# Two transformer layers on one core: feed-forward products from two 12-bit float32 parts, the value matrix laid out through DRAM, the ternary weights prepared first

## The chip, the cores and the metric

The kernel runs on one core of one Trainium2 chip. The metric is the device time of one execution in microseconds (us), lower is better. A core has a matrix engine (TensorE, PE in the profile; PEld is its weight load, which runs beside the products), a vector engine (VectorE, DVE), an engine for activation functions and copies (ScalarE, ACT), GpSimd (POOL), and SyncE (SP), which here issues all DMA transfers. Work lies in SBUF, 128 partitions wide; products land in PSUM, eight banks of 128 x 512 float32.

## What is computed

Sixteen batches of 256 tokens with 256 features pass through two layers. After each of the four sublayers the input is added and the sum is normalised (`x = _layernorm(x + f(x))`):

```python
# 1: mixing in the Fourier domain, 16 heads of 16
qf, kvf = fft(x @ W_q.T), fft(x @ W_kv.T)          # each divided by its norm
values = ifft(qf * cumsum(kvf, axis=1)).real;  out = values @ W_o.T
# 2: eight small experts, the best one of each token by a gate
out = (1 - sel_scale) * x + sel_scale * (bias + degen_up)
# 3: attention, 16 heads of 16; the 256 x 768 projection is only reshaped to (3, 16, 256, 16)
Q, K, V = (x @ W_qkv.T).reshape(b, 3, H, L, D_H)   # per batch
out = softmax(Q @ K.T / 4) @ V @ W_o.T
# 4: feed-forward, 1024 wide, with weights rounded to three levels in groups of 64
w1, w2 = ternary(W_fc), ternary(W_proj)
h = square(relu(x @ w1.T));  out = (h * rsqrt(mean(h**2) + eps)) @ w2.T
```

Three levels times a bfloat16 scale: each weight of the fourth sublayer has few significant bits. Inputs, outputs and all matrix products of the kernel before are float32.

## The kernel before

Sublayers 1 and 2 of a batch are `front`, sublayer 4 is `back`. Attention runs for four batches at a time: `attention(i)` for the groups i = 0 to 3, batch g of a group on the partitions 32g to 32g+15.

The order of the instructions is made when the program is built. Every operation is entered with the tiles that it reads and writes, a cost in us for each engine that may do it, and a priority (`order.prio`; a smaller number goes first). A planner (`Order.run`) keeps a clock for every engine, takes at each step the operation that can start earliest, among near equals the one with the smaller priority, gives it a buffer, and fixes its place in its engine's queue. Every engine then runs its queue in that order. Buffers are few: eight PSUM banks (at most six for attention, two for the work beside it), thirteen 512-wide `work` tiles, four `x` tiles for the inputs.

The main loop first folds the Fourier matrices into the projections (`fold`, L417 to L451), then runs the four fronts of group 0. For each group it then enters the attention of group i, and beside it the four backs of group i-1 and the four fronts of group i+1, which fill gaps. After group 0's attention has been entered, `ternaries` (L465 to L489) turns the two feed-forward weights into three levels; its loads wait for `begun`, a mark that a score product of group 0 sets. The last four backs come at the end.

`attention` in steps: the projection products (L759) into a bank, for blocks of 32 tokens. VectorE transposes each block (L768) into the tile `zt`, whose three thirds are Q, K and V; the marks `zq`, `zr`, `zv` and `turn` stand for those parts and for the turn of the group. A row of ones is written beside K by DMA (L776). V is turned once more on TensorE (L793) and evacuated into `v`, 32 columns a head and batch, zeros in the unused ones (L342 and L343, the shared evacuation on ScalarE or VectorE). First pass: scores (L810), whose row maxima VectorE takes (L819); a DMA writes the maxima beside Q (L827). Second pass, head by head: scores with the maxima subtracted (L844), the exponential on ScalarE into tiles in the V third of `zt` (L853), the products with V (L859), then transpose, division and store into `o` (L867, L871). At the end the output projection (L901).

`back`: the input is transposed on TensorE (L521) and evacuated. The first product (L925) goes into a bank in four parts of two blocks of 128; each part passes through relu (L933), a square (L936 on ScalarE or L937 on VectorE), and a second square for the mean (L941). VectorE sums the second squares over the eight blocks in one reduction (L949). The second product (L959) has the transposed hidden values as its stationary operand; a product with a column of ones (L968) sums the squares over the partitions. Normalisation (from L535) and the output DMA (L983) follow.

Of the kernel before, what the change touches and what calls it, by code (L numbers as in the profile page):

```python
# [11 lines left out]
BF16 = mybir.dt.bfloat16  # L12
AF = mybir.ActivationFunctionType
# [17 lines left out]
ZQ = H * S  # L31
LN_EPS = 1e-5
# [5 lines left out]
C_ALL = C_INV + 2 * 2 * P  # L38


def constants():
# [12 lines left out]
    inv = np.zeros((2, HD, 8))  # L54
    for k in range(8):
# [5 lines left out]
        inv[1, :, k] = (1 + alt) / 16 if k == 0 else -si / 16  # L61
        c[k::8, C_MK : C_MK + 3] = (0, 0, 1) if k == 0 else (1, -1, 0)
    ft = np.zeros((H, HD, 2, H, 8))
    iv = np.zeros((2, H, HD, H, 8))
# [4 lines left out]
    iv = iv.reshape(2, 2, P, P)  # L69
    for e in range(2):  # L70
        c[:, C_FT + e * 256 : C_FT + (e + 1) * 256] = ft[e]
        for m in range(2):
            at = C_INV + (m * 2 + e) * P
            c[:, at : at + P] = iv[m, e]
# [11 lines left out]
LAG = {PE: 0.27, DVE: 0.2, ACT: 0.25, POOL: 0.2, SP: 2.4}  # L86
SLACK = {PE: 0.15, DVE: 0.1, ACT: 0.1, POOL: 0.1, SP: 0.0}
SWITCH = 0.13
LATER = 15.0
# [46 lines left out]
class Order:  # L136
# [65 lines left out]
    def run(self):  # L202
# [5 lines left out]
        clock = {e: 0.0 for e in LAG}  # L208
        mode = None
# [3 lines left out]
        while ready:  # L213
# [42 lines left out]
            clock[e] = at + (cost if e != SP else 0.06)  # L256
# [18 lines left out]
def forward(ctx, tc, x, xt, wq, wkv, wo0T, f0, degen, cs, wqkvT, wo1T, wfc, wproj, cst, out):  # L275
# [3 lines left out]
    pp = ctx.enter_context(tc.tile_pool(name="pp", bufs=1, space=PSUM))  # L279
    order = Order(tc)  # L280
# [13 lines left out]
    zq, zv, zr = fixed(zt_), fixed(zt_), [fixed(zt_), fixed(zt_)]  # L294
    begun = fixed(zt_)
# [4 lines left out]
    at = 3328  # L300
# [3 lines left out]
    for i in range(13):  # L304
        order.slot("work", place(f"work{i}", [P, 512]))
    for i in range(2 * GB):
        order.slot("x2", place(f"x2_{i}", [P, 512]))
    for tag, bufs, n in (
        ("x2T", 1, 2 * GB * S), ("x", 4, 512), ("h", 1, 2048), ("sq", 1, 2048), ("oT", 1, 2048), ("pd", 3, 512), ("f", 2, 272), ("c2", 2, 128),
        ("mk", 1, 144), ("mT", 1, 256), ("st", 34, 16), ("st64", 6, 64), ("nm", 2, 64), ("nmT", 2, 128),  # L310
    ):
        for i in range(bufs):
            order.slot(tag, place(f"{tag}{i}", [P, n]))
    for i in range(2):
        order.slot("wb", place(f"wb{i}", [P, 512], BF16))
        order.slot("sb", place(f"sb{i}", [P, 8], BF16))
    order.slot("lane", *[None] * 4)
    order.limit = {("ps", "r"): 2, ("ps", "a"): 6, ("lane", "r"): 2}
    v = const("v", [P, 2 * H, GB, 32])
    o = const("o", [P, S // 32, D])  # L320


    def load(dst, src, dst_tile, prio=None):
        return op((SP, 0.1, lambda: nc.sync.dma_start(dst(), src)), [dst_tile], [], prio=prio)
# [37 lines left out]
    wqs = fixed(zt_[:, 1280:2304].rearrange("p (s c d) -> p s c d", s=2, c=2))  # L362
    wos = fixed(zt_[:, 2304:2816].rearrange("p (c d) -> p c d", c=2))
    f0s = fixed(zt_[:, 2816:3104].rearrange("p (c f) -> p c f", c=2))
    rows = fixed(zt_[0:NE, 3104:3240])
# [688 lines left out]
```

## Time and profile before

| What | us |
|---|---|
| Median of three runs (932.14, 940.5, 941.45) | 940.5 |
| Profiled execution, its own time | 940.41 |
| Its span, first to last instruction | 938.6 |
| Fronts of group 0 end, the projection of group 0 begins | 106.3 |
| Projection of groups 1, 2, 3 begins | 310.0, 487.3, 694.7 |
| Output projection of group 3 begins | 863.7 |

A row of the profile's groups names a line of the kernel, an engine, an operation, the tile written and the tiles read with their shapes, the number of instructions, their busy time together, the mean time of one in ns, and the idle time of the engine just before them with what ended it. Instructions of one engine overlap, so the mean of one can be longer than the busy time divided by the count. A release by "issue" is time in which the engine waited for nothing that the profile shows. The granted clock (PEclk) is the share of TensorE's full clock that the chip allowed.

### The profile page before, as it was taken

Reading aid. Unit: us, or ns where it says so; the run is one execution under the profiler, and the core shown is the slowest. Engines: PE = TensorE matmul, PEld = TensorE weight load, DVE = VectorE, ACT = ScalarE, POOL = GpSimd, SP = SyncE. Lnnn points to the kernel's source line nnn. Section 1 sums busy time; section 2 is a strip of 40 time slices with the busy share of each in tenths; the row PEclk is TensorE's granted clock in tenths of the full one; section 3 lists DMA queues with packets and bytes.
Section 4 is the critical chain, followed back from the end, with each engine's and each line's share of the span. In section 5 each row is a group of like instructions: output and inputs, shape, how many; then the busy total and the mean of one; then the engine's idle time right before and its main releaser. Section 6 shows DMA issues by size and latency. Waiting matters only on the chain.

```text
span 938.6 us, 14746 instructions
## 1 busy us (share of the span) xinstructions
PE 870.9 (93%) x5678; PEld 609.5 (65%) x5678; DVE 662.6 (71%) x1449; ACT 425.9 (45%) x845; POOL 146.1 (16%) x334
## 2 busy tenths in 40 slices
PE   7777999949899999999989999999999999999996
PEld 4554678525568676676556777766667778545885
DVE  1868799897577998858659898566689794313553
ACT  4826110536646213675661435495632226454542
POOL 1122100365112001012102001012120001000201
PEclk9978795578899998999999999999999899656998
DMA  5101030000000000011000000000000000000000
GB/s 181 54 12 45 2 96 11 2 1 2 22 23 13 11 15 14 13 35 36 12 13 3 1 25 25 1 24 12 2 1 4 2 14 24 12 1 1 1 23 23
DMA packets 18874, 19.01 MB, mean 20 GB/s; under 512 B 2092, under 2 KB 17780, under 8 KB 18804
## 3 DMA queue, kind: packets, MB, share of 16 engines
q1 hardware_dynamic: 18804, 18.07, 6.4%
q8 instruction: 44, 0.72, 0.3%
q14 instruction: 26, 0.21, 0.1%
HBM read 13.35 MB, written 4.19 MB: 19 GB/s over the span
## 4 chain that ended last, share of the span: by engine, by line
PE 79%; DVE 13%; ACT 5%; issue 1%; POOL 1%; DMA 0%; DVEq 0%; SPq 0%; ACTq 0%; POOLq 0%
PE bank L925 13%; PE bank L959 11%; PE bank L759 9%; PE bank L810 8%; PE bank L844 7%; PE bank L859 7%; PE bank L575 5%; PE bank L654 3%; PE bank L901 3%; DVE nm L819 3%; PE bank L521 3%; DVE work L949 2%; PE bank L731 2%; PE bank L620 2%; PE bank L675 1%; PE bank L793 1%
## 5 line engine op out<-in xcount | busy, mean ns | idle before, releaser
L853 ACT ACTIVATE zt<-bank 128x512 f32<-128x512 f32 x256 | 135.3, 607 | 91.9 <-PE bank L844 91.8
L819 DVE TENSOR_REDUCE nm<-bank 128x2 f32<-128x512 f32 x256 | 157.4, 680 | 12.6 <-PE bank L810 12.2
L959 PE MATMUL bank<-w2T,h 128*128 128x256 f32 x512 | 120.9, 387 | 2.6 <-DVE work L738 2.6
L925 PE MATMUL bank<-work,w1T 128*128 128x256 f32 x512 | 121.6, 390 | 1.4 <-ACT work L342 1.4
L529 POOL TENSOR_SCALAR st<-st 128x2 f32<-128x2 f32 x80 | 17.1, 214 | 609.7 <-DVE st L537 388.0
L959 PEld LDWEIGHTS bank<-w2T,h 128*128 128x128 f32 x512 | 96.0, 192 | 21.9 <-issue 4.3
L925 PEld LDWEIGHTS bank<-work,w1T 128*128 128x128 f32 x512 | 96.7, 194 | 20.4 <-issue 2.4
L844 PE MATMUL bank<-zt 17*128 17x256 f32 x1024 | 101.0, 488 | 6.7 <-ACT zt L853 5.8
L810 PE MATMUL bank<-zt 16*128 16x256 f32 x1024 | 97.1, 457 | 0.4 <-DVE nm L819 0.4
L859 PE MATMUL bank<-zt,v 128*32 128x256 f32 x1024 | 94.2, 478 | 3.3 <-ACT zt L853 3.3
L844 PEld LDWEIGHTS bank<-zt 17*128 17x128 f32 x1024 | 63.8, 229 | 41.0 <-issue 21.3
L933 ACT ACTIVATE work<-bank 128x512 f32<-128x512 f32 x64 | 37.9, 594 | 115.4 <-PE bank L925 115.3
L768 DVE STREAM_TRANSPOSE zt<-bank 128x1024 f32<-128x1024 f32 x64 | 84.4, 1447 | 7.4 <-PE bank L759 7.4
L759 PE MATMUL bank<-wqr,x2T 128*128 128x512 f32 (+1 forms) x256 | 83.7, 487 | 0.0
L810 PEld LDWEIGHTS bank<-zt 16*128 16x128 f32 x1024 | 67.5, 210 | 24.6 <-issue 13.4
L759 PEld LDWEIGHTS bank<-wqr,x2T 128*128 128x128 f32 x256 | 48.9, 191 | 33.7 <-issue 30.3
L859 PEld LDWEIGHTS bank<-zt,v 128*32 128x32 f32 x1024 | 33.9, 127 | 48.9 <-issue 30.6
L949 DVE TENSOR_REDUCE work<-sq 128x256 f32<-128x2048 f32 x16 | 59.1, 3696 | 7.1 <-ACT sq L941 7.1
L575 PE MATMUL bank<-wf,x 128*128 128x512 f32 x128 | 60.8, 611 | 0.1
L867 DVE STREAM_TRANSPOSE work<-bank 128x512 f32<-128x512 f32 x32 | 22.6, 708 | 52.8 <-PE bank L859 52.8
L530 POOL TENSOR_TENSOR st<-st,mhalf 128x2 f32<-128x2 f32 x80 | 57.1, 716 | 5.4
L535 DVE BATCH_NORM_STATS2 st<-work 128x6 f32<-128x256 f32 x120 | 45.2, 414 | 0.4
(171 smaller groups left out, 1164.8 us busy)
## 6 DMA issues: line engine op xcount, KB each, us to landing
x<-in_xT SPq DMA_DIRECT2D x16, 256.0 KB, 2.8
x<-in_x SPq DMA_DIRECT2D x16, 256.0 KB, 2.8
out<-work SPq DMA_DIRECT2D x16, 256.0 KB, 2.1
work<-in_wfc SPq DMA_DIRECT2D x4, 256.0 KB, 4.4
work<-in_wproj SPq DMA_DIRECT2D x4, 256.0 KB, 5.5
wqr<-in_wqkvT SPq DMA_DIRECT2D x1, 768.0 KB, 6.6
zt<-in_cst SPq DMA_DIRECT2D x1, 512.0 KB, 3.9
zt<-nmT SPq DMA_DIRECT2D x32, 8.0 KB, 1.8
```

Source lines behind the costliest of these rows:

```text
L530: pool([dst], [dst, mhalf], 0.7, lambda: G.tensor_tensor(dst.v, dst.v, a(mhalf)[:, 0:n], ALU.pow))
L575: T.matmul(pb.v.rearrange("p a s k -> p (a s k)"), xT.v[:, c, ts(t, P)], a(wf)[:, c].rearrange("p a s f -> p (a s f)"), start=(c == 0), st ...
L759: T.matmul(b.v.rearrange("p j d -> p (j d)"), x2T.v[:, c, tb].rearrange("p g k -> p (g k)"), a(wqr)[:, c, j0 * HD : (j0 + nj) * HD], start ...
L768: lambda b=b, tb=tb, j0=j0, nj=nj: V.transpose(ztv[:, j0 : j0 + nj, ts(tb, 32)], b.v.unsqueeze(2).to_broadcast([P, nj, 2, HD])),
L810: T.matmul(sc[g].v[:, t, :], part(g, HD, 0, h, t * P, P), part(g, HD, 1, h), start=True, stop=True,)
L819: lambda nm=nm, sc=sc, g=g, h=h: V.tensor_reduce(nm.v[:, g, h % 8, :], sc[g].v, AX.X, ALU.max, negate=True),
L844: T.matmul(sc[g].v[:, c, :], part(g, HD + 1, 1, h, c * P, P), part(g, HD + 1, 0, h), start=True, stop=True,)
L853: act([e], [sc[g]], 512, lambda e=e, sc=sc, g=g: A.activation(e.v, sc[g].v, AF.Exp, scale=HD ** -0.5))
L859: T.matmul(av.v[32 * g : 32 * g + 32, hk, :], a(v)[:, h * 2 + c, g, :], es[g].v[:, c, :], start=(c == 0), stop=(c == 1),)
L925: T.matmul(pb.v[:, i, :], a(w1T)[:, c, ts(q * 2 + i, P)], xT.v[:, c, :], start=(c == 0), stop=(c == 1))
L949: (DVE, 2.2, lambda: V.tensor_reduce(acc.v, sq.v.rearrange("p k s -> p s k"), AX.X, ALU.add)),
L959: T.matmul(pw.v[:, t, :], h.v[:, k, ts(t, P)], a(w2T)[:, k, :], start=(k == 0), stop=(k == HID // P - 1))
```

## The change

Float32r is a type of 32 bits of which the matrix engine takes a shortened mantissa; the change declares the feed-forward weights and four new tiles in it.

- **Feed-forward.** The input and the hidden values are each split into a high part (a copy into a float32r tile) and a low part (the value minus the high part). Each product becomes two, one with each part, summed in the same bank. The second squares are added part by part into one tile, then halves are added, in place of the one reduction. `h`, `sq` and one `work` tile give way to `xs`, `hi` and `lo`.
- **V.** Only the blocks up to the sixth are still transposed into `zt`. The blocks from the sixth on are evacuated into a `work` tile, written to DRAM by SP (six writes a group), and read back by SP into `v` in its final layout (four reads a group, pieces of 16 values). The turn on TensorE is gone, `v` has 17 columns a head and batch, and the projections of the last two blocks no longer wait for the group's turn, at a priority 2 lower.
- **Ternary weights.** Entered before the first attention, in tiles that share memory with `o` and `oT`; their loads have priority -8.5, ahead of `wqr` and `wo1`. GpSimd takes no part; the steps that subtracted and added the weight again are gone; a maximum is joined to a multiplication.
- **Prologue.** Two loads of constants in place of one, all four transposed inputs first, the untransposed inputs of group 0 not loaded; nine products on a tile of ones at the start (`warm`); `fold` in two parts with two more matrices. The early fronts form two products in place of the masked ones and add the input, and the bias of the gate, on TensorE.
- **Planner.** New costs for DMA issue and transfer, for some VectorE operations, and for the new products.

```diff
-LAG = {PE: 0.27, DVE: 0.2, ACT: 0.25, POOL: 0.2, SP: 2.4}
+LAG = {PE: 0.27, DVE: 0.2, ACT: 0.25, POOL: 0.2, SP: 0.3}
...
+ISSUE = 0.43
+MOVE = 1.2
...
-            clock[e] = at + (cost if e != SP else 0.06)
+            clock[e] = o.end
+            if e == SP:
+                clock[e] = at + ISSUE
+                o.end = moved = max(at + ISSUE + 1.6, moved + cost)
...
-    for i in range(13):
+    for i in range(12):
         order.slot("work", place(f"work{i}", [P, 512]))
...
+    for i in range(2):
+        order.slot("xs", place(f"xs{i}", [P, 2 * 512], F32R))
+    for tag in ("hi", "lo"):
+        order.slot(tag, place(tag, [P, 2048], F32R))
...
-    w1T, w2T = const("w1T", [P, 2, HID]), const("w2T", [P, HID // P, D])
+    w1T, w2T = fixed(place("w1T", [P, 2, HID], F32R)), fixed(place("w2T", [P, HID // P, D], F32R))
...
+    def warm():
+        b = ps([P, P], "p")
+        def go():
+            for n in range(9):
+                T.matmul(b.v, a(ones), a(ones), start=True, stop=True)
+        pe([b], [ones], 2.5, go, prio=-20.0)
...
+        if early:
+            one, two = w(P, 2, S), w(P, 2, S)
+            dve([one], [qT, cu, *extra], 512, lambda: V.tensor_tensor(one.v, qT.v, cu.v, ALU.mult))
+            dve([(two, 0)], [qT, cu, *extra], 256, lambda: V.tensor_tensor(two.v[:, 0, :], qT.v[:, 0, :], cu.v[:, 1, :], ALU.mult))
+            dve([(two, 1)], [qT, cu, *extra], 256, lambda: V.tensor_tensor(two.v[:, 1, :], qT.v[:, 1, :], cu.v[:, 0, :], ALU.mult))
...
+                    for n, (l, g) in enumerate((
+                        (one.v[:, 0, at], a(gi)[:, 0, :]), (one.v[:, 1, at], a(ge)[:, 0, :]),
+                        (two.v[:, 0, at], a(ge)[:, 1, :]), (two.v[:, 1, at], a(ge)[:, 1, :]),
+                    )):
+                        T.matmul(y.v[:, t, :], l, g, start=(n == 0), stop=False)
+                    for c in range(2):
+                        T.matmul(y.v[:, t, ts(c, P)], xT.v[:, c, at], ident, start=False, stop=(c == 1))
...
+                if tb >= 5:
+                    st = tile_("work", [P, nj * HD])
+                    evacuate(lambda st=st: st.v, lambda b=b: b.v.rearrange("p j d -> p (j d)"), st, b, nj * HD)
+                    op(
+                        (SP, 0.1, lambda st=st, tb=tb, j0=j0, nj=nj: nc.sync.dma_start(
+                            vd.slot.ap[:, tb * 32 - VT : tb * 32 - VT + 32, j0 * HD : (j0 + nj) * HD], st.v
+                        )),
+                        [(vd, (tb, j0))], [st],
+                    )
+        for g in range(GB):
+            op(
+                (SP, 0.1, lambda g=g: nc.sync.dma_start(
+                    va[:, :, g, 0:HD],
+                    vd.slot.ap[g].rearrange("t e -> (t e)")[2 * ZQ * HD - VT * NJ * HD :].rearrange("(n p d) -> p n d", p=P, d=HD),
+                )),
+                [(v, g)], [vd],
+            )
...
+        act([(xs, 0)], [bx], 512, lambda: A.copy(xs.v[:, 0], bx.v))
+        dve([(xs, 1)], [bx, (xs, 0)], 512, lambda: V.tensor_tensor(xs.v[:, 1], bx.v, xs.v[:, 0].bitcast(F32), ALU.subtract))
...
-                    for c in range(2):
+                    for n in range(4):
                         T.matmul(
-                            pb.v[:, i, :], a(w1T)[:, c, ts(q * 2 + i, P)], xT.v[:, c, :], start=(c == 0), stop=(c == 1)
+                            pb.v[:, i, :], a(w1T)[:, n // 2, ts(q * 2 + i, P)], xs.v[:, n % 2, n // 2, :],
+                            start=(n == 0), stop=(n == 3),
                         )
...
+            act([(hi, q)], [h], 512, lambda h=h, part=part: A.copy(part(hi), h.v))
+            act([sq], [h], 512, lambda h=h, sq=sq: A.activation(sq.v, h.v, AF.Square))
+            dve([(lo, q)], [h, (hi, q)], 512, lambda h=h, part=part: V.tensor_tensor(part(lo), h.v, part(hi).bitcast(F32), ALU.subtract), us=0.69)
+            if q:
+                dve([acc], [acc, sq], 512, lambda sq=sq: V.tensor_tensor(acc.v, acc.v, sq.v, ALU.add), us=0.69)
...
+                        for n, part in enumerate((hi, lo)):
+                            T.matmul(
+                                pw.v[:, t, :], part.v[:, k, ts(t, P)], a(w2T)[:, k, :],
+                                start=(k + n == 0), stop=(k + n == HID // P),
+                            )
...
+    order.prio = 90.0
+    ternaries()
     for i in range(NG):
         order.prio = 100.0 * (i + 1)
         attention(i)
-        if i == 0:
-            order.prio = 105.0
-            ternaries()
```

## The prediction

> **What bounds the kernel now.** I read the page's engine line first, then the busy time of each engine by stage (the cuts lie where the first projection product of each group of four batches starts, and where its score passes begin and end), then the groups of instructions, the timeline of the tail, ten-microsecond windows for the clock, and the DMA queues.
>
> ```profile
> span 938.6 us, 14746 instructions
> ## 1 busy us (share of the span) xinstructions
> PE 870.9 (93%) x5678; PEld 609.5 (65%) x5678; DVE 662.6 (71%) x1449; ACT 425.9 (45%) x845; POOL 146.1 (16%) x334
> ```
> TensorE leaves 67.7 us of the span idle; VectorE is second. By stage (columns: length, busy time of PE, PEld, DVE, ACT, POOL with counts, granted clock, DMA share, GB/s):
>
> ```profile
> core 0: us, PE busy (x) PEld busy (x) DVE busy (x) ACT busy (x) POOL busy (x), PEclk, DMA share, GB/s
> 14.30:106.30 92.00, 71.56 (x268) 48.67 (x268) 63.43 (x216) 49.82 (x101) 15.96 (x41) 0.84 0.11 32
> 106.30:184.00 77.70, 77.38 (x490) 54.36 (x490) 72.23 (x114) 14.57 (x33) 6.56 (x5) 0.70 0.11 33
> 184.00:224.00 40.00, 25.38 (x204) 14.32 (x206) 38.94 (x62) 18.26 (x34) 28.50 (x25) 0.71 0.01 1
> 224.00:310.00 86.00, 80.56 (x519) 58.14 (x512) 57.50 (x177) 51.97 (x105) 16.21 (x49) 0.93 0.06 16
> 310.00:487.30 177.30, 170.44 (x1264) 114.69 (x1263) 138.41 (x307) 88.52 (x181) 20.03 (x54) 0.97 0.07 20
> 487.30:694.70 207.40, 202.58 (x1444) 144.40 (x1443) 157.90 (x358) 103.13 (x209) 31.94 (x92) 0.99 0.04 11
> 694.70:804.80 110.10, 109.85 (x675) 81.86 (x673) 83.50 (x114) 34.77 (x65) 7.47 (x20) 0.95 0.03 9
> 804.80:863.70 58.90, 58.31 (x477) 28.21 (x478) 13.12 (x32) 31.66 (x62) 1.29 (x4) 0.54 0.02 6
> 863.70:938.60 74.90, 65.97 (x321) 57.86 (x319) 37.03 (x69) 29.65 (x53) 14.08 (x40) 0.96 0.04 15
> ```
> From 310 on TensorE is never idle for long: a pass taken from it there shortens the span until VectorE takes over. Two stages differ: 184 to 224 is the preparation of the ternary weights (DVE 38.9 of 40 us, PE waits), and 804.8 to 863.7 is attention alone, at a granted clock of 0.54. The groups that the change halves (form, then busy us, mean ns, idle before):
>
> ```profile
> L959 PE MATMUL bank<-w2T,h 128*128 128x256 f32 x512 | 120.9, 387 | 2.6 <-DVE work L738 2.6
> L925 PE MATMUL bank<-work,w1T 128*128 128x256 f32 x512 | 121.6, 390 | 1.4 <-ACT work L342 1.4
> ...
> L949 DVE TENSOR_REDUCE work<-sq 128x256 f32<-128x2048 f32 x16 | 59.1, 3696 | 7.1 <-ACT sq L941 7.1
> ```
> A back calls 16 products in each of its two matrix products; over 16 backs that is 256 a line, so each float32 product shows as two instructions of 237 ns of busy time (120.9 / 512 and 121.6 / 512). In the tail, weight loads and products of one back in the timeline:
>
> ```profile
> 871.83 6.77 PEld L925 LDWEIGHTS bank<-work,w1T 128*128 128x128 f32 x32 [0.91 <-ACT work L342]
> 871.83 7.17 PE L925 MATMUL bank<-work,w1T 128*128 128x256 f32 x32 [0.68 <-ACT work L342]
> ```
> The loads run wholly beside the products.
>
> **The change part by part**, on the profiled run's own time, 940.41 us = the span 938.6 + 1.8 around it; the median of the three runs is 940.5, so nothing is to be shifted.
>
> *Feed-forward products.* Each float32 product becomes two float32r products (with the high and the low part). The trace has no float32r. Upper bound: each costs what both instructions of a float32 product cost, 474 ns. Lower: half of one instruction, 118 ns. Between them: one instruction, 237 ns. I take 118: on the chain 8 instructions of 256 columns (L925) and 4 of 512 (L575) both take 1.73 us, 0.84 ns a column, so the time is all streaming, and an operand that is handed over as a short part should need neither the second instruction nor the second half of the first, if splitting a long operand is what these are for. That is inferred, and both other values are rivals. The weight load does not stop this: 16 transposes, each with a 128-column load of its own, take 1.90 us on the chain (L793), 119 ns each. So 1024 x 118 = 121 us in place of 242.5: TensorE -121.
>
> *What the splitting costs.* Per back four subtractions for the low part, one for the input, three sums and a half-width one: VectorE, priced by L937 (691 ns) and L628 (421 ns), 8 x 0.69 + 0.42 = 5.9 us, 95 over all; L949's 59.1 goes. ScalarE: four more copies by L941's 628 ns, +40 over all; the input's copy replaces one there now.
>
> *V through DRAM.* Out: 128 transposes (PE 15.6, L793), their evacuations (ACT 10.8, DVE 1.3), a quarter of L768 (60.3 + 32.3, so DVE -23.2). In: 24 evacuations by L342/L343 (half each, some 7 us an engine), 24 writes and 16 reads on SP. SP's issues cost 0.4 us and up to 0.6 for L776; 40 more, 16 to 24 us of SP over the run, hidden under a queue that mostly waits; behind them stand x loads, the row of ones and nmT. Each read has 4096 pieces of 64 bytes, 256 on each of 16 engines. Bounds: by bytes, as x<-in_x (256 KB, 2.8 us), 11 us a group; by pieces, at the mean packet here:
>
> ```profile
> q1 hardware_dynamic: 18804, 18.07, 6.4%
> ```
> 6.4% of 16 x 938.6 us over 18,804 packets is 51 ns of mostly 1 KB, so 13 us a read, 52 a group. The cover is the first score pass: from the end of L759 to the first big L844, 39, 63, 56 and 70 us. Even at the upper end only group 0 waits, 52 + 3 for the writes - 39 = 16 us, with the fronts of group 1 to fill it. I take 0, and 16 into the range. The Trainium skill (DMA: Bandwidth & Descriptors, Specifications) puts the least transfer for line rate at 512 bytes, with read-modify-write below; no run here shows 64-byte pieces, and by that the 52 could be exceeded, which is a rival.
>
> *Ternary weights ahead of group 0.* Their VectorE work was 46.6 us (L467 to L478); after, one 8-wide step less and no GpSimd step between: 0.66 + 0.29 + 2 x 0.16 + 4 x 0.69 = 4.0 each, 32. They leave 184 to 224 and compete in the prologue; eight loads of 256 KB move ahead of wqr and wo, at 4.4 to 5.5 us to landing, far before 106.
>
> *Prologue.* Four early fronts: DVE -2.5 each (five products and a subtraction become three, two adds go into PSUM), PE + 3.5 each (four 256-column products at 0.43, four of 128 at 0.3, two of 136 at 0.3); one more pair of folds, 1.9; the warm-up products lie under the first load (PE waits to 5.4). x loads for fronts 2 and 3 no longer wait for slots (SP waited 58.8 us there at the longest). PE 80.4 + 14 + 2 + 7 (L489) = 103; DVE 64 - 10 + 32 = 86. Bounds 95 (the present 0.84 clock near 1) to 120; I take 101, -5.
>
> Totals: PE 871 - 121 - 16 + 16 = 750; DVE 663 - 59 - 23 - 15 - 10 - 1 + 95 + 7 = 657; ACT about 461.
>
> *By stage.* 106 to 310: PE 183 - 10 - 4 - 7 = 162, and the 20 us of idle, mostly the ternary wait, fall to 8: 170, -34. 310 to 694.7: PE 373 - half of L925 and L959 there (105.3 / 2) - 7.8 = 312; DVE 296 - 26 - 12 + 41 + 3 = 302. Two engines at nearly equal load do not overlap to 97%, as PE does now; I take 0.91, between that and 224 to 310's 0.94 on one side and the prologue's 0.78 on the other: 342, -43. 694.7 to 863.7: PE 168 - 30 - 4 = 134, DVE 101, cold at its end as now: 143, -26. Tail: a back now takes 14.7 us of PE, after it 7.6, while ScalarE needs 10 (relu, square, copy, square at 0.6, four times) and VectorE 9: 4 x 10 + 8 + 11 = 59, -16. Sum -124: span 815, time 816.
>
> **The rivals.**
> *The clock falls (chance 0.15, 856).* Two windows, the first of attention among fronts, the second of attention alone:
>
> ```profile
> 440.00:450.00 10.00, 8.67 (x77) 4.96 (x79) 7.32 (x24) 9.36 (x21) 1.97 (x6) 1.00 0.17 54
> ...
> 820.00:830.00 10.00, 10.00 (x84) 4.90 (x88) 1.40 (x3) 4.54 (x10) 0.00 (x0) 0.50 0.01 2
> ```
> PE is busy throughout the second, yet granted half. With the clock, 16 score products take 2.02 us instead of 1.15, and 16 value products 1.87 instead of 1.07: 16 heads cost 41 us a group more. Half the dense feed-forward work goes, so the narrow products stand alone more often; if half of groups 1 and 2 turn cold, +40. Against it: dense work stays at 60% of PE in those groups. The Trainium skill (TensorE: Matmul & The Clock Gate, The HAM clock gate) ties the clock to how busy the PE has been; by that alone a stage 100% busy would stay at full clock, and this trace disagrees, 0.50.
>
> *float32r streams like a float32 instruction (0.05, 930 to 937).* At 237 ns the 121 us return, less some of the idle that is now counted.
>
> *The V pieces (0.04, slower).* Second pass waits for all four reads. With a mean cover of 57 us, the price of a piece at which the 124 us are eaten is (57 + 124 / 4) / 1024 = 86 ns; at 200 ns a group needs 205, 148 beyond cover, 592 in all, of which some 250 of fronts and backs can move in: about 1150.
>
> *float32r costs as much as float32 (0.02, slower).* 474 ns each: +364, 1180.
>
> *More than forecast (0.08, 755).* PE packed at 97% with attention kept warm: 750 / 0.97 less 20.
>
> **How the numbers follow.** Forecast 0.66, 775 to 851 by its own bounds: PE packed at 97% (750 / 0.97), and the prologue at 120 with the 16 us of group 0's reads added. Range: 765 to 868, from part of the low case over the cold clock. One per cent, 9 us, is what this measurement can tell. Within 1%: 0.03 (most of the 237-ns case); slower 0.06; faster 0.91.
>
> **What would show it.** L925 and L959 together 1024 instructions near 118 ns of busy time, PE near 750; no group like L949, VectorE near 657; no 40-us stretch with PE at 6 tenths after the prologue; the first V read landing before the first score pass ends; attention at 1.00 in groups 1 and 2, 0.5 only late in group 3. The forecast is wrong if VectorE, not TensorE, ends the chain in groups 1 and 2, if PE's sequencer or weight loads hold f32r above 150 ns, or if POOL or SP rows stand on the chain.

## The result, and the profile after

The changed kernel takes 838.1 us (median of four runs, 833.9 to 842.0) where the kernel before, beside it, takes 940.3: a ratio of 0.893, 95% interval 0.886 to 0.900. The prediction was 816 us, in a range from 765 to 868. The profiled execution took 842.0 us, 840.2 of them its span; against the 940.4 of before that is 98 us less, where the sum of the stages had 124. In what follows the changed kernel's later control run (834.0 us, 833.1 to 841.9) stands beside the experiments. In the sessions of the experiments the kernel before ran at 911 to 917 us or at 932 to 942, and its runs above and its profile are all of the longer kind, so the 98 and the stages below flatter the change: against the shorter runs, some 916 us, the control takes 82 us less, a ratio of 0.914 (0.902 to 0.926). Where an experiment is compared with the kernel before, it is with the 916.

The head of the page of the changed kernel:

```profile
span 840.2 us, 14851 instructions
## 1 busy us (share of the span) xinstructions
PE 784.6 (93%) x5656; PEld 565.4 (67%) x5656; DVE 637.8 (76%) x1531; ACT 457.2 (54%) x916; POOL 123.5 (15%) x305
```

TensorE still fills 93% of the span. It lost 86.3 us of work (870.9 - 784.6), not the 121 forecast; VectorE and ScalarE came out within 3% of the forecast 657 and 461. The stages, cut where the first projection product of each group starts (prologue, groups 0, 1, 2, 3, tail), in the columns used before:

```profile
0.00:93.40 93.40, 80.09 (x389) 60.10 (x389) 68.41 (x227) 54.58 (x114) 15.90 (x37) 0.92 0.26 85
93.40:254.40 161.00, 156.72 (x1119) 107.88 (x1120) 126.17 (x305) 77.39 (x159) 18.90 (x52) 0.86 0.17 27
254.40:447.80 193.40, 185.08 (x1335) 129.27 (x1335) 149.90 (x357) 109.01 (x220) 28.90 (x68) 0.89 0.16 30
447.80:642.00 194.20, 181.89 (x1359) 129.70 (x1359) 150.23 (x364) 104.56 (x213) 28.00 (x77) 0.90 0.16 23
642.00:774.00 132.00, 130.29 (x1131) 91.56 (x1129) 98.31 (x178) 76.77 (x147) 14.93 (x32) 0.92 0.19 27
774.00:840.20 66.20, 50.57 (x328) 46.92 (x328) 44.76 (x104) 34.92 (x68) 16.83 (x40) 0.86 0.05 17
```

| stage | before | after | change | forecast |
|---|---|---|---|---|
| prologue | 106.3 | 93.4 | -13 | -5 |
| group 0 | 203.7 | 161.0 | -43 | -34 |
| groups 1 and 2 | 384.7 | 387.6 | +3 | -43 |
| group 3 | 169.0 | 132.0 | -37 | -26 |
| tail | 74.9 | 66.2 | -9 | -16 |

Groups 1 and 2, the stretch in which the forecast let TensorE set the time, gave nothing. A little of that is only where the work lies: 56 feed-forward instructions that before ran within group 0 now run in group 1, and 16 went from group 2 to group 3; the 39 more are about 6 us at the measured price. The rest, some 40 us, is the question.

The groups of instructions that matter (form, then busy us, mean ns, idle before):

```profile
L873 PE MATMUL bank<-zt 16*128 16x256 f32 x1024 | 127.1, 522 | 1.9 <-DVE nm L882 1.9
L907 PE MATMUL bank<-zt 17*128 17x256 f32 x1024 | 90.6, 426 | 1.1 <-ACT zt L916 0.7 <-DVE nm L882 0.2
L922 PE MATMUL bank<-zt,v 128*32 128x256 f32 x1024 | 80.1, 393 | 6.3 <-ACT zt L916 6.3
L1029 PE MATMUL bank<-w2T,hi 128*128 128x256 f32 x256 | 77.1, 328 | 3.8 <-ACT hi L1017 3.4 <-ACT work L611 0.4
L1029 PE MATMUL bank<-w2T,lo 128*128 128x256 f32 x256 | 74.1, 317 | 3.7 <-DVE lo L1019 3.7
L1000 PE MATMUL bank<-xs,w1T 128*128 128x256 f32 x512 | 70.6, 291 | 1.2 <-DVE xs L990 1.2
...
L882 DVE TENSOR_REDUCE nm<-bank 128x2 f32<-128x512 f32 x256 | 157.4, 679 | 17.6 <-PE bank L873 17.4
```

and two of them in the kernel before:

```profile
L810 PE MATMUL bank<-zt 16*128 16x256 f32 x1024 | 97.1, 457 | 0.4 <-DVE nm L819 0.4
...
L819 DVE TENSOR_REDUCE nm<-bank 128x2 f32<-128x512 f32 x256 | 157.4, 680 | 12.6 <-PE bank L810 12.2
```

The 1024 score products of the first pass, which the change does not touch, cost 30 us more than before (127.1 against 97.1). The maxima over those scores cost VectorE the same 157.4 us in both kernels, 39.4 us a group. Both facts meet in the stretches where the first passes lie. Here they are, from the first to the last maximum of each group (to 2 us), before and then after:

```profile
128.00:170.00 42.00, 41.68 (x321) 35.23 (x321) 41.88 (x74) 6.33 (x16) 0.00 (x0) 0.61 0.18 58
332.00:392.00 60.00, 58.88 (x429) 42.01 (x421) 53.83 (x97) 21.10 (x43) 3.90 (x11) 0.94 0.05 15
518.00:576.00 58.00, 57.93 (x457) 43.05 (x456) 52.81 (x87) 21.55 (x42) 4.00 (x12) 1.00 0.03 11
718.00:776.00 58.00, 58.00 (x420) 43.86 (x417) 49.77 (x78) 17.05 (x33) 3.09 (x8) 0.91 0.02 6
```

```profile
116.00:158.00 42.00, 41.60 (x286) 32.59 (x288) 41.21 (x73) 3.67 (x9) 0.00 (x0) 0.61 0.46 53
274.00:324.00 50.00, 49.66 (x352) 38.18 (x351) 45.34 (x82) 12.01 (x23) 2.58 (x6) 0.72 0.42 50
468.00:520.00 52.00, 51.49 (x365) 38.85 (x361) 47.31 (x82) 12.39 (x25) 0.90 (x2) 0.72 0.44 42
662.00:714.00 52.00, 51.08 (x424) 39.04 (x421) 47.23 (x83) 24.53 (x46) 1.28 (x2) 0.89 0.39 43
```

Compare each length with VectorE's busy time, the third pair. Together the four stretches took 218 us before, with VectorE busy for 198; after, 196 us, with VectorE busy for 181. VectorE is busy for 91 and 92% of their length, which shrank by 22 us where VectorE's work in them shrank by 17. TensorE looks just as full (216 of 218, 194 of 196), yet its content changed. The same stretches with the feed-forward lines alone hold 349 of their 1024 instructions before, 87.4 us (L925 41.0, L959 46.3), and 264 after, 42.1 us (L1000 23.5, L1029 18.6). An instruction there fell from 250 ns to 159, so some 349 x 0.091 = 32 us of the 87 that the change saved in these products (242.5 - 155.8) were saved where VectorE is full. What is left to TensorE there are mostly narrow products, and the granted clock of the first passes of groups 1 and 2 fell from 0.94 and 1.00 to 0.72. In a ten-microsecond window within it:

```profile
310.00:320.00 10.00, 10.00 (x64) 7.78 (x57) 9.91 (x20) 1.09 (x2) 1.30 (x4) 0.50 0.03 11
```

TensorE shows no idle time, VectorE next to none. Four heads are 64 score products and 16 maxima: 8.1 us of TensorE at half clock (2.02 us for 16) and 9.8 us of VectorE (157.4 / 256 each). Which of the two sets the pace can't be seen in this row, where a TensorE at half clock counts as busy. The timeline of the same ten microseconds tells more. Here are the weight loads of the score products, 16 at a time, and the maxima (start us, us, then the instruction; in brackets how long the engine was idle before it, and what ended that):

```profile
311.51 2.29 PEld L873 LDWEIGHTS bank<-zt 16*128 16x128 f32 x16 [0.43 <-DVE nm L882]
313.38 2.48 DVE L882 TENSOR_REDUCE nm<-bank 128x2 f32<-128x512 f32 x4
314.12 2.29 PEld L873 LDWEIGHTS bank<-zt 16*128 16x128 f32 x16 [0.33 <-DVE nm L882]
315.99 2.48 DVE L882 TENSOR_REDUCE nm<-bank 128x2 f32<-128x512 f32 x4
316.74 2.29 PEld L873 LDWEIGHTS bank<-zt 16*128 16x128 f32 x16 [0.33 <-DVE nm L882]
```

The loads of 16 scores take 2.3 us at this clock, but they start 2.6 us apart, each time after a wait that a maximum ended: four maxima (2.5 us) and the small operations between them set the pace here, with TensorE 0.3 us behind. Whether that holds for the time of the whole kernel is what the experiments are about.

### The profile page after: what moved, and what is told of

It reads as the page before. It is cut to its first block, busy times and chain, and to the rows that moved or that the text cites. A ratio compares the mean times of both kernels' runs of the same rounds, so it can differ in the third digit from the quotient of the medians.

```text
span 840.2 us, 14851 instructions
## 1 busy us (share of the span) xinstructions
PE 784.6 (93%) x5656; PEld 565.4 (67%) x5656; DVE 637.8 (76%) x1531; ACT 457.2 (54%) x916; POOL 123.5 (15%) x305
## 4 chain that ended last, share of the span: by engine, by line
PE 75%; ACT 12%; DVE 9%; POOL 2%; issue 2%; DVEq 0%; ACTq 0%; POOLq 0%
PE bank L873 13%; PE bank L815 10%; PE bank L907 8%; PE bank L922 7%; PE bank L1029 7%; PE bank L603 6%; PE bank L1000 4%; PE bank L702 3%; PE bank L964 2%; DVE nm L882 2%; ACT zt L916 2%; PE bank L648 2%; PE bank L726 2%; ACT work L1009 2%; ACT work L1018 2%
## 5 line engine op out<-in xcount | busy, mean ns | idle before, releaser
L882 DVE TENSOR_REDUCE nm<-bank 128x2 f32<-128x512 f32 x256 | 157.4, 679 | 17.6 <-PE bank L873 17.4
L873 PE MATMUL bank<-zt 16*128 16x256 f32 x1024 | 127.1, 522 | 1.9 <-DVE nm L882 1.9
L873 PEld LDWEIGHTS bank<-zt 16*128 16x128 f32 x1024 | 89.1, 240 | 30.2 <-DVE nm L882 16.0
L907 PE MATMUL bank<-zt 17*128 17x256 f32 x1024 | 90.6, 426 | 1.1 <-ACT zt L916 0.7
L922 PE MATMUL bank<-zt,v 128*32 128x256 f32 x1024 | 80.1, 393 | 6.3 <-ACT zt L916 6.3
L1029 PE MATMUL bank<-w2T,hi 128*128 128x256 f32 x256 | 77.1, 328 | 3.8 <-ACT hi L1017 3.4
L907 PEld LDWEIGHTS bank<-zt 17*128 17x128 f32 x1024 | 59.1, 196 | 27.4 <-issue 15.4
L1029 PE MATMUL bank<-w2T,lo 128*128 128x256 f32 x256 | 74.1, 317 | 3.7 <-DVE lo L1019 3.7
L1000 PE MATMUL bank<-xs,w1T 128*128 128x256 f32 x512 | 70.6, 291 | 1.2 <-DVE xs L990 1.2
L1000 PEld LDWEIGHTS bank<-xs,w1T 128*128 128x128 f32 x512 | 64.4, 193 | 8.6 <-issue 3.8
L824 DVE STREAM_TRANSPOSE zt<-bank 128x1024 f32<-128x1024 f32 (+1 forms) x48 | 64.6, 1458 | 4.5 <-PE bank L815 3.9
L1029 PEld LDWEIGHTS bank<-w2T,hi 128*128 128x128 f32 x256 | 56.6, 221 | 10.7 <-ACT hi L1017 4.4
L1029 PEld LDWEIGHTS bank<-w2T,lo 128*128 128x128 f32 x256 | 56.5, 221 | 6.3 <-DVE lo L1019 5.7
L922 PEld LDWEIGHTS bank<-zt,v 128*32 128x32 f32 x1024 | 31.6, 110 | 40.6 <-ACT zt L916 16.3
L364 ACT COPY work<-bank 128x512 f32<-128x512 f32 (+1 forms) x34 | 17.4, 514 | 66.2 <-PE bank L815 57.4
```

The costliest lines, as they stand in the source:

```text
L824: lambda b=b, tb=tb, j0=j0, nj=nj: V.transpose(ztv[:, j0 : j0 + nj, ts(tb, 32)], b.v.unsqueeze(2).to_broadcast([P, nj, 2, HD])),
L873: T.matmul(sc[g].v[:, t, :], part(g, HD, 0, h, t * P, P), part(g, HD, 1, h), start=True, stop=True,)
L882: lambda nm=nm, sc=sc, g=g, h=h: V.tensor_reduce(nm.v[:, g, h % 8, :], sc[g].v, AX.X, ALU.max, negate=True),
L907: T.matmul(sc[g].v[:, c, :], part(g, HD + 1, 1, h, c * P, P), part(g, HD + 1, 0, h), start=True, stop=True,)
L922: T.matmul(av.v[32 * g : 32 * g + 32, hk, :], v_part(g, h * 2 + c), es[g].v[:, c, :], start=(c == 0), stop=(c == 1),)
L1000: T.matmul(pb.v[:, i, :], a(w1T)[:, n // 2, ts(q * 2 + i, P)], xs.v[:, n % 2, n // 2, :], start=(n == 0), stop=(n == 3),)
```

## The experiments

The first theories, by their letters in the expectations: A, VectorE holds the first score passes, and in one experiment part of the tail, so that products taken out there save little; B, the feed-forward products are themselves on the path, so each that goes is worth its busy time; C, the route of V through DRAM costs what it saves; D, less dense work lets the clock fall, and narrow products pay it back. Theory E came after the first eight runs and makes A definite: VectorE's maxima set the length of the first passes, and what is taken from TensorE there is lost.

**The feed-forward change alone, and all but it.** First the kernel before with nothing but the split products (V packed in 17 columns, to make room), then, with the lines below turned round but V left as it is, the changed kernel with the float32 products of before:

```diff
-    v = const("v", [P, 2 * H, GB, 32])
+    v = const("v", [P, 2 * H * GB * (HD + 1) + 31 - HD])
...
-                    for c in range(2):
+                    for n in range(4):
...
-                            pb.v[:, i, :], a(w1T)[:, c, ts(q * 2 + i, P)], xT.v[:, c, :], start=(c == 0), stop=(c == 1)
+                            pb.v[:, i, :], a(w1T)[:, n // 2, ts(q * 2 + i, P)], xs.v[:, n % 2, n // 2, :],
+                            start=(n == 0), stop=(n == 3),
```

> The kernel before with the split float32r feed-forward alone (and V packed in 17 columns, for room in SBUF; the product that sums the squares takes its bank from attention's six). Theory A, the first score pass is held by VectorE, so that products taken out of it save little: some 50 to 65 us less than before, 875 to 890. Theory B, TensorE holds every stage and only the products' own duration (152 ns a product in place of my 118) is off: 87 us less, about 853. Theory C, the missing time went into the new route of V: this kernel does not have it, so the full 121 of my sum comes back, about 820 to 830.

> The changed kernel with the float32 feed-forward of before, sums of squares in one reduction again. A: 890 to 900, the feed-forward being worth some 55 us. B: 925, since 242.5 - 156 = 87 us of products come back. C: above 930, since the other parts would then be worth next to nothing.

Alone: 894.4 us (893.0 to 898.7), 22 less than the 916. Left out: 863.5 us (862.5 to 864.5), 29.5 more than the changed kernel's 834.0. Both lie outside every range expected: even theory A, the nearest, gave the split products 50 to 65 us. TensorE's busy time differs by 48.5 us there (826.8 against 778.3 in the control), not by 87: the float32 version keeps the clock at 0.944, against 0.901, and its first-pass products take 99.7 us, against 127.2. The split products are worth 22 to 30 us of the change's 82.

**The products with the low parts left out**, 512 of the 1024:

```diff
-                    for n in range(4):
+                    for n in range(2):
...
-                        for n, part in enumerate((hi, lo)):
...
-                                pw.v[:, t, :], part.v[:, k, ts(t, P)], a(w2T)[:, k, :],
+                            pw.v[:, t, :], hi.v[:, k, ts(t, P)], a(w2T)[:, k, :],
```

> The changed kernel with the products with the low parts left out (512 of the 1024); all VectorE and ScalarE work stays. B, TensorE is the bound throughout: its 78 us of busy time go, time about 765. A, the products lie partly under VectorE's first pass: 25 to 45 us less, 795 to 812. C: nothing more than B says, since V's route is not touched.

830.0 us (829.8 to 833.3): 4 us less, for half of 156 us of products; theory B had 765, A 795 to 812. The mean granted clock fell to 0.847, the first-pass products rose to 141.6 us, and TensorE's busy time fell by 23 us only (778.3 to 755.5). Theory B, by which each product is worth its busy time, is out, and A's size missed too.

**The sums of squares on GpSimd:**

```diff
-                dve([acc], [acc, sq], 512, lambda sq=sq: V.tensor_tensor(acc.v, acc.v, sq.v, ALU.add), us=0.69)
+                pool([acc], [acc, sq], 1.3, lambda sq=sq: G.tensor_tensor(acc.v, acc.v, sq.v, ALU.add))
...
```

> The changed kernel with the sums of the squares on GpSimd in place of VectorE (39 us of VectorE work moved; GpSimd is 85% idle). A: VectorE holds the first pass and part of the tail, 8 to 25 us less, 813 to 830. B: no change beyond 1%. If GpSimd and VectorE slow each other, slower than 838.

835.9 us (831.3 to 837.2): no difference, as theory B had it and A (813 to 830) had not. But the experiment took much less from VectorE than meant. The moved sums were 39 us (L1021 32.7, L1022 6.7), and its busy time fell by 9 (637.7 to 629.1), and other operations of it became longer, the subtractions for the low part first (the control, then this run):

```profile
L1019 DVE TENSOR_TENSOR lo<-work,hi 128x512 fp32r<-128x512 f32 x64 | 43.2, 683 | 4.1 <-ACT hi L1017 3.9
...
L1019 DVE TENSOR_TENSOR lo<-work,hi 128x512 fp32r<-128x512 f32 x64 | 54.6, 869 | 5.7 <-ACT hi L1017 5.7
```

So it does not decide whether the work that the change gave VectorE holds the time. The sums lie in the backs besides, not among the maxima, so it says nothing about VectorE in the first passes.

**The changed kernel as a control, and with V by the old route:**

```diff
-                if tb >= 5:
-                    st = tile_("work", [P, nj * HD])
...
+                zs = ([zq, *zr] if tb <= 5 else []) + ([zv] if tb >= 5 else [])
...
-                    va[:, :, g, 0:HD],
...
+                    T.transpose(b.v[:, k, :], zt_[:, 2 * ZQ + (n + k) * P : 2 * ZQ + (n + k + 1) * P], ident)
```

> The changed kernel again, beside the others of this call: 838 within 5 us.

> The changed kernel with V by the old route (all blocks transposed on VectorE, 128 transposes on TensorE, no DRAM). By my sum (PE 15.6, DVE 23): 10 to 20 us more, 848 to 858. Theory D, the clock, says less, because the transposes are dense work and keep the clock up: 838 to 848. If the reads in 64-byte pieces hold the second pass (theory C): faster than 838.

The old route takes 857.9 us (853.4 to 863.6), within the 848 to 858 of the sum and above theory D's 838 to 848, so V through DRAM is worth some 24 us. Theory C is out.

**Dense products put among the first-pass scores**: one, then two float32 products of 128 x 128 x 256 ahead of each of the 64 groups of 16 scores. Their results are overwritten.

```diff
...
+                    for n in range(2):
+                        T.matmul(sc[0].v[:, 0, :], a(wqr)[:, 0, 0:P], a(wqr)[:, 1, 0:S], start=True, stop=True)
...
```

> The changed kernel with one dense float32 product of 128 x 128 by 256 columns, 0.43 us, ahead of each of the 64 score groups of the first pass; its result is overwritten, the order of all other work is the same. Theory D: the granted clock depends on dense work, and the first pass and the short feed-forward products in it run at half clock for want of it; with 27.6 us of products added the clock of the first pass rises from 0.5 to 0.8 or more and the time falls, 822 to 836. Theory B, TensorE's own work is the bound: 27 us more, 865. Theory A, the first pass is held by VectorE whatever the clock: 838 to 845.

> The same with two such products, 55 us of TensorE work added. D: clock of the first pass near 1.0, 820 to 840, no slower than the changed kernel. B: 893. A: 840 to 855.

One product: 854.4 us (853.1 to 857.4), clock 0.901. Two: 846.6 us (845.2 to 847.8), clock 0.957. So 64 more products, 18 us of busy time (68.7 against 50.7), made it 8 us shorter: the clock is worth time, and the second product raised it where the first had hardly done so (first passes at 0.67 to 0.93, the control's at 0.62 to 0.91). But theory D had 822 to 836 for one and 820 to 840 for two, no slower than the changed kernel, and both came out slower; of the ranges expected only A's 840 to 855 for two was met. The first passes of the kernel with two say more (cut in the same way as above, as are those of the other runs below):

```profile
116.00:160.00 44.00, 42.66 (x367) 28.80 (x362) 41.21 (x73) 3.84 (x9) 0.00 (x0) 1.00 0.43 51
274.00:328.00 54.00, 53.69 (x434) 38.12 (x434) 47.70 (x86) 13.53 (x27) 2.57 (x6) 0.99 0.44 48
468.00:522.00 54.00, 53.93 (x431) 38.72 (x432) 47.16 (x81) 12.09 (x24) 0.78 (x2) 1.00 0.44 39
666.00:722.00 56.00, 55.63 (x488) 42.25 (x487) 48.03 (x84) 24.95 (x47) 1.27 (x2) 1.00 0.43 39
```

The clock is full throughout, the first scores are a third cheaper (86.1 us against 127.2 in the control), and with the 68.7 us of added products TensorE's part grew by 27.6 us. The four stretches grew by 10, against the control's

```profile
sum 198.00, PE 195.50 PEld 148.70 DVE 183.80 ACT 52.58 POOL 5.14; mean PE 48.87 PEld 37.18 DVE 45.95 ACT 13.14 POOL 1.28
```

With one product TensorE's part grew by 108.2 + 50.7 - 127.2 = 31.7 us, the stretches by 18. VectorE's busy time in them is 184 to 187 us in all three. So TensorE had room for a part of the added work, though it shows next to no idle time in the control. At full clock its own work in the four stretches is about 206 - 69 = 137 us, VectorE's 184: a faster clock alone could not bring them far below their 198. This is where theory E came from.

**Maxima over half of the keys**, in the changed kernel, then the same with the float32 products of before:

```diff
-                        [(nm, (h, g))], [sc[g]], 512,
-                        lambda nm=nm, sc=sc, g=g, h=h: V.tensor_reduce(nm.v[:, g, h % 8, :], sc[g].v, AX.X, ALU.max, negate=True),
+                        [(nm, (h, g))], [sc[g]], 256,
+                        lambda nm=nm, sc=sc, g=g, h=h: V.tensor_reduce(nm.v[:, g, h % 8, :], sc[g].v[:, :, 0:P], AX.X, ALU.max, negate=True),
```

> The changed kernel, with the maximum that shifts the exponentials taken over the first half of the keys only: the 256 maxima of VectorE read 256 elements instead of 512; the products stay. In the changed kernel the 64 maxima of a group take 39.4 us of VectorE (157.4 us / 4), and the first score passes last 42, 50, 52 and 52 us with VectorE 90 to 98% busy in them, while TensorE's 16 x 16 score products need 18 us at full clock and 32 at half. Theory E (VectorE's maxima set the length of the first passes, so that what is taken from TensorE there is lost): the maxima fall to some 22 us a group, then TensorE's 32 us at half clock come next, 7 to 15 us less a group: 775 to 808 us against the changed kernel's 834. Theory D (TensorE at half clock sets them, the maxima run beside it): 825 to 840.

> The float32 feed-forward products of before in the changed kernel (as in e2_ffn_f32), with the maximum over the first half of the keys only (as in e7_half_max). With all keys the split products are worth 29.5 us (863.5 - 834.0). Theory E: with short maxima the stretches that VectorE held become TensorE's, so the split products are worth more: this kernel lies 40 to 70 us above e7_half_max, at 830 to 855. Theory D: the worth stays near 30, or falls as less dense work makes the first passes colder: 20 to 35 us above e7_half_max.

The planner is told of the shorter maximum too, so the order of the other work changes with it. 795.3 us (791.3 to 796.9), within theory E's 775 to 808 and below theory D's 825. The first passes:

```profile
114.00:146.00 32.00, 31.39 (x293) 25.22 (x293) 29.16 (x82) 2.39 (x5) 0.00 (x0) 0.81 0.63 79
254.00:298.00 44.00, 43.76 (x364) 30.52 (x363) 34.73 (x94) 17.24 (x32) 3.36 (x10) 0.88 0.53 69
442.00:484.00 42.00, 42.00 (x405) 31.41 (x405) 36.12 (x101) 21.10 (x42) 4.24 (x11) 0.96 0.63 72
622.00:664.00 42.00, 41.85 (x388) 32.01 (x389) 32.81 (x86) 20.75 (x38) 2.84 (x6) 0.90 0.56 56
```

160 us in all, 38 less than the control's 198, and the time fell by 39: nearly the whole gain lies there. Nothing was taken from TensorE, yet its busy time fell from 778.3 to 735.1: as many of its instructions as before (1450, in the control 1448) now run in the shorter stretches, the mean clock rises (0.928), and the first-pass products fall to 83.8 us. So the low clock was here at least in part a consequence of the wait on VectorE. With the float32 products it takes 841.1 us (838.0 to 842.9), 45.8 more: the same feed-forward change that is worth 29.5 us under long maxima is worth 45.8 under short ones, as theory E had it (40 to 70).

**First scores for half of the keys too:**

```diff
-                                sc[g].v[:, t, :], part(g, HD, 0, h, t * P, P), part(g, HD, 1, h),
+                                sc[g].v[:, t, 0:P], part(g, HD, 0, h, t * P, P), part(g, HD, 1, h, 0, P),
...
```

> The changed kernel, with the maxima and also the first score products for the first half of the keys only: 256 maxima over 256 elements and 1024 products of 128 columns instead of 256. Theory E: VectorE's 22 us a group still set the first passes, which fall from 49 to some 28 us on the average: 834 - 4 x 21 = 750, within 735 to 775. Theory D: half of the 127 us of first score products goes, and some of it comes back as a lower clock elsewhere: 775 to 805. Either way group 0's V reads, which land some 5 us before its second pass now, may be waited for: 10 to 15 us, once.

772.7 us (764.5 to 778.8), 61 less than the control. The median lies within theory E's 735 to 775, but the runs reach across its border with theory D's 775 to 805, so this one does not tell the two apart. Two of its first passes:

```profile
256.00:294.00 38.00, 36.37 (x369) 28.22 (x368) 36.00 (x98) 16.99 (x31) 2.49 (x6) 0.91 0.65 74
422.00:458.00 36.00, 35.29 (x397) 28.73 (x397) 32.32 (x88) 17.52 (x34) 1.99 (x6) 0.95 0.59 62
```

The four take 138 us, 60 less than the control's. This is the shortest of all the kernels here. A softmax does not depend on the shift, so its result is that of the reference as long as no score of the other half of the keys lies so far above the shift that its exponential overflows; the guarantee that the largest exponent is zero is what it gives up.

**The kernel before with the maxima over half of the keys**, the edit of above in L819:

> The kernel before, with the maximum over the first half of the keys only, as in e7_half_max; nothing of the change. Theory E: the maxima hold the changed kernel more than the one before, whose first passes have TensorE busy for 58.9 of 60, 57.9 of 58 and 58 of 58 us with the float32 feed-forward products among them, so it gains less than the changed kernel's 39 us: 13 to 27 us, to 911 to 925, and the whole change is then worth 116 to 130 us (this less 795) where it is worth some 104 with all keys. If the maxima have nothing to do with the size of the change, this kernel gains the same 39 us: about 899, and the change stays at 104.

884.4 us (881.2 to 885.8), 32 less than the 916, a ratio of 0.967 (0.963 to 0.972). Neither expected time was met; both were counted from 938 us, and as a gain the 32 lies between theory E's 13 to 27 and the 39 of the other answer. So the maxima held the kernel before nearly as much as the changed one. The whole change under short maxima is worth 884.4 - 795.3 = 89 us, 7 more than under long ones, where theory E had 12 to 26 more. So the maxima explain why feed-forward work that was taken out of the first passes brought little; they explain little of the size of the whole change. The feed-forward part grows by 16 us and the whole by 7, so the other parts must together be worth some 9 us less under short maxima, a difference of four medians with a few us of doubt in each. That the parts which relieve VectorE, the V route first, are the ones that lose is an argument; it was not run.

## The prediction, step by step

The span came out at 840 us where the sum had 815, inside the range, but not by the way forecast. Groups 1 and 2 missed by 46 us. The prologue, group 0 and group 3 together gave 28 more than forecast and the tail 7 less, and a part of the 28 was luck, as group 3 shows below. And the forecast was for 124 us off a time of 940; of the 916 the change took 82.

*The price of a product (118 ns).* The step from row to price was right, its use as a mean was not. Products of one back at full clock, then at half, in the timeline (start us, us, then the instruction):

```profile
552.16 0.28 PE L1029 MATMUL bank<-w2T,hi 128*128 128x256 f32 x1
552.28 0.29 PE L1029 MATMUL bank<-w2T,lo 128*128 128x256 f32 x1
552.40 0.28 PE L1029 MATMUL bank<-w2T,hi 128*128 128x256 f32 x1
...
718.67 0.41 PE L1029 MATMUL bank<-w2T,hi 128*128 128x256 f32 x1
718.88 0.41 PE L1029 MATMUL bank<-w2T,lo 128*128 128x256 f32 x1
719.10 0.41 PE L1029 MATMUL bank<-w2T,hi 128*128 128x256 f32 x1
```

They start 0.12 us apart at full clock and 0.21 apart at half. But they come in runs of eight or sixteen, and each run's first and last product count longer, so that in a window at clock 1.00 (550 to 560) 32 take 4.58 us, 143 ns each; with the runs at half clock the mean is 155.8 / 1024 = 152 ns (L1000 70.6, L1029 85.2 where its two rows overlap). The term came out at 156 us where the sum had 121. Beside each product lies a weight load nearly as long (4.02 us for the 32 in that window), so the trace does not show which of the two sets the 0.12 us.

*TensorE's total (750).* It is 784.6. The 35 us are the feed-forward term (+35) and the first scores, at a lower clock and waiting (+30), less what L907 and L922 lost (101.0 to 90.6 and 94.2 to 80.1) and some 6 us elsewhere.

*310 to 694.7 (-43): the step that failed.* It took half of L925 and L959 off TensorE, saw VectorE at 302 of 312 us, and met the near balance with a packing factor of 0.91 for the whole stage. The loads do not lie evenly in it. In the first passes VectorE is busy for 91% of the time, and 87 of the 242 us of feed-forward products lay in those of the three later groups, where a shorter product shortens little; outside them the span fell from 720.6 to 644.2 us, 76 of the 98, with what the prologue, the ternary weights and the clock of group 3 gave among it. What the prediction named as a sign against itself, VectorE ending the chain in groups 1 and 2, did not show: over the whole span the chain gives L873 13% and L882 2%. A TensorE at half clock is still busy when the maximum ends, and so, it seems, the chain runs through it. The timeline of the first pass and the maxima experiments show the wait, the chain does not.

*Attention at 1.00 in groups 1 and 2* was wrong: 0.50 in the window shown. So the rival "the clock falls" came in part, with its sign and on the first scores +30 us of its 40, though not as a cause by itself: with a full clock bought by two dense products for each group of 16 scores the kernel was 12.6 us slower, and shorter maxima raised the clock without it.

*Splitting on VectorE (+95 - 59) and ScalarE (+40)* was right in its totals (L990, L1019, L1021 and L1022 together 93 us). Whether any of it ends the time stays open, since the sums on GpSimd took only 9 us from VectorE.

*V through DRAM, hidden.* The four reads of group 0 are issued from 130.5 on, the DMA engines are at rest again from about 145, and its second pass starts at 153; no DMA stands among the releasers of L907 and L922 above. The price of a piece was far off the bound taken:

```profile
q1 hardware_dynamic: 86820, 26.20, 16.4%
```

The queue's share of 16 engines is 0.164 x 16 x 840.2 = 2205 us, 1244 more than before's 961, over 65,536 pieces: at most 19 ns each, where the sum's bound had 51. The Trainium skill (DMA: Bandwidth & Descriptors, Specifications) puts line rate at transfers of 512 bytes and more. The trace agrees that such pieces move fewer bytes: 64 in 19 ns are 3.4 GB/s an engine, where the 18.07 MB in 18,804 packets of before, at 51 ns each, are 19. But 19 ns is far from 86, the price at which it would have eaten the gain. SP's share was mis-sized the other way: a read's issue takes 2.3 us (median), not 0.4 to 0.6, four in 9.0 us; the first maxima's writes, which stand behind them, went out from 139.6 on, ahead of the second pass. The route is worth 24 us, more than the 15.6 of TensorE's turn; with the old one TensorE is busy for 30 us more than in the control (808.5 against 778.3) and VectorE for 22 (659.4 against 637.7), and which of the two counts was not separated.

*Prologue and ternary weights.* Prologue and group 0 gave 56 us where 39 was forecast, 8 of them by moving feed-forward work on; the stretch of 40 us with TensorE waiting for the ternary weights is gone (in group 0 TensorE is busy for 156.7 of 161.0 us). Which part gave the 9 us beyond was not tried.

*Group 3* gave 37 for 26. The forecast left its end cold, but it came out warm: the same narrow products, alone from 744 on as before from 805, at full clock:

```profile
750.00:760.00 10.00, 10.00 (x156) 5.74 (x152) 3.19 (x7) 9.62 (x20) 0.00 (x0) 1.00 0.07 23
```

The window 820 to 830 of before has 84 instructions of TensorE, at 0.50. The second pass of group 3 took 61.9 us of TensorE before (L844 31.5, L859 30.4) and takes 43.5 (L907 23.4, L922 20.1): 18 of the 37 us, which no term of the sum held. Why it is warm now is not shown.

The *tail* gave 9 for 16: TensorE works 50.6 of its 66.2 us, so the chain of copies and squares in it is longer than the 59 worked out.

*The other rivals.* float32r at 237 or 474 ns is excluded by the timeline, slow V pieces by the queue, 755 by the 838.

## What to carry over

Before a saving on the busiest engine is counted, cut the stage where another engine's row is at 90% and count what of the saving lies inside those cuts; over a third of this one did. An engine at half clock looks full, so "busy 10.00" at a clock of 0.50 is no proof that it sets the pace: the waits of its weight loads in the timeline hint at it, and halving the other engine's work, or adding work to this one, tells in one run. The Trainium skill (VectorE: DVE Perf Modes, Rules for kernel authors) calls the reduction VectorE's slowest operation and advises to restructure it on a hot path. These runs agree with the advice (39 us for maxima over half of the keys, 61 with their scores), not with the ranking: a reduction over 512 elements takes 680 ns, a TENSOR_TENSOR over as many 683 (L1019 of the control).

## What the runs showed of the hardware

- Dense work and the granted clock: 64 float32 products put among the first scores (50.7 us of busy time) left the mean clock at 0.901, 128 (68.7 us) raised it to 0.957, and to 1.00 in the first passes. Taking 512 products out lowered it from 0.901 to 0.847, so that TensorE's busy time fell by 23 us and the time by 4.
- Neither a busy TensorE nor the kind of its products fixes the clock alone: the narrow products of group 3's second pass ran for 50 us at 0.50 before (810 to 860) and for 26 us at 1.00 after (744 to 770), TensorE busy throughout in both.
- A float32r product of 128 x 128 x 256 starts every 0.12 us at full clock, a quarter of the 474 ns that both instructions of a float32 product were busy.
- A maximum over 512 elements takes VectorE 680 ns, over 256 elements 415: about 1.04 ns an element and 150 ns that don't shrink.
- VectorE beside GpSimd: with the sums of squares on GpSimd, VectorE's subtractions took 869 ns in place of 683, and of 39 us moved 9 were gained on it.
- A DMA of 4096 pieces of 64 bytes holds SP for 2.3 us at its issue, six times what a plain one does (0.37), while its pieces cost at most 19 ns each.
